# A four-layer graph network on one core: dinv as a row by 32x32 squares and two transfers, fewer state turns on TensorE, and a last mix and store chunk by chunk

## The chip, the cores and the metric

The kernel runs on one core of a Trainium2 chip. Time is device microseconds (us) of one execution, and the time of a kernel is the median over several executions. The core's engines work side by side, each through its own queue in order: TensorE (PE) multiplies and can turn (transpose) a 128x128 square, VectorE (DVE) and ScalarE (ACT) work element by element, GpSimd (POOL) does a few small operations here, and SyncE (SP) issues nearly all transfers, which land some time after their issue.

## The reference

32 graphs share one 512x512 adjacency matrix; each has 512 nodes of 128 features, in float32. There are four layers, each of the form x = x + layer(relu(layernorm(x))):

```python
# layer 0: graph convolution
A_hat = adj + eye(n); d = A_hat.sum(-1) ** -0.5
out = (d[:, None] * A_hat * d[None, :]) @ h @ W.T + b
# layer 1: gated graph network, five steps (in_matrix = out_matrix = adj)
m = adj @ h;  av = concat([m, m])
z = sigmoid(av @ w3.T + b3 + h @ u3.T + c3)
r = sigmoid(av @ w4.T + b4 + h @ u3.T + c3)
hv = tanh(av @ w5.T + b5 + (r * h) @ u5.T + c5)
h = (1 - z) * h + z * hv
# layers 2 and 3: graph attention, softmax over the edges
h = x @ W; e = leaky_relu((h @ a_src)[:, None] + (h @ a_dst)[None, :])
out = softmax(where(edge, e, -inf)) @ h        # layer 2: elu(out)
```

## The kernel before, in words

**An order laid out by a planner.** The program never writes its instructions down directly. `op` (line 61) notes an operation with its engine, an assumed cost, a due time and what it reads and writes. `Plan.run` (line 92) then plays the whole list through a model of the five engines (`attempt`, line 154): each engine takes, among its ready operations whose buffers are free, the one with the smallest due. A due is replaced by a smaller one if the chain of work behind an operation is long; the pairs in `ends` (line 305) say by how much, several are tried, and the order with the earliest end is emitted. So each engine's order is fixed when the program is built, and on the chip each engine waits in that order. `near_end` is the planned time after which a second way of setting dues applies. `IDLE_FROM` allows PE filler turns late in the plan; the profile shows none.

**Graphs in pairs.** Graphs are taken two at a time. `begin(b)` runs layer 0 for b and b+1 (`gcn`), `ggnn` the five steps of layer 1, and `attention` layers 2 and 3 (`gat`). Six lanes of graphs are in work at once, so that PE has other graphs' work while one waits. The planner takes one unit of due for 10.3 us (SLOT).

**Layer 0.** Graphs 0 to 3 (`first`) use the adjacency as it is: `product` (line 659) multiplies the four chunks of y by the rows of adjT, and adds the identity either by a fifth piece of 128 columns per chunk (graph 0, `by_diag` false) or by taking the diagonal block from `diag`, in which the identity has been added on DVE (graphs 1 to 3). dinv, the inverse square root of the degrees, is folded into the normalization and the output. Later pairs use the normalized matrix anT made by `normalized` (line 677). For that dinv is needed as a row along the free dimension: line 685 turns the four columns of dinv, each spread over 128 columns, into a PSUM bank `drow`, and four operations on DVE (line 690) multiply adjT by the column and the row, four more (line 693) fix the diagonal. `right_factors` (line 399) makes four combined blocks of a matrix on DVE, for the `products` of a pair (line 604), which take 28 instructions of 256 columns (line 628) for two graphs.

**Layer 1.** A state is kept as features by nodes (hT). Each step needs it as nodes by features (h) as well. There are two ways. By PE: `to_features` (line 554) does four turns (line 560) into a bank, and ACT copies them out (line 796). By squares: `shuttle` (line 564) lets DVE turn 32x32 squares (lines 570 and 574), SP writes them out in four transfers `far<-sq` (line 577), and one or two more, `h<-far` (line 581), read them back with the squares in place. `EARLY` (line 23) says from which due on (line 789) states go by squares. `FAR0`, `FAR1` (line 24) say for which graphs the very first state is turned that way (`shuttle_first`, line 589, four transfers out and four back), and not by PE and an ACT copy (line 746).

**Layers 2 and 3.** For the last four graphs (`near`) attention avoids transfers. Its last part mixes: for each of four blocks j, `mix_from` (line 903) multiplies e[j] into all four chunks c of the output, two chunks to a bank. Then for each bank a reciprocal (line 917), for layer 3 two scaled additions (line 925), and a store of two chunks (line 947).

Of the kernel before, what the change touches and what calls it, by code (L numbers as in the profile page):

```python
# [22 lines left out]
EARLY = 8  # L23
FAR0, FAR1 = 2, 4
# [231 lines left out]
def gnn_stack(ctx: ExitStack, tc: tile.TileContext, a: dict, out: bass.AP):  # L256
# [48 lines left out]
    }, [(179, 0.06), (175, 0.06), (177, 0.12)], 1350,  # L305
# [52 lines left out]
    op("DVE", 0.2, -15, lambda: nc.vector.tensor_scalar_add(b0.t, b0.t, -1.0), w=[b0])  # L358
# [6 lines left out]
    for l, w in ((2, "L2_gnn_W"), (3, "L3_gnn_w")):  # L365
        w_aug[l] = fixed([P, D + 3], f"w_aug{l}", 2)
        op("SP", 0.45, -990.5, lambda l=l, w=w: nc.sync.dma_start(w_aug[l].t[:, :D], a[w]), w=[w_aug[l][0]], delay=3.4)
        a_pair[l] = fixed([P, 2], f"a_pair{l}", 2)
        for i, k in enumerate(("src", "dst")):
            op("SP", 0.45, -990.4, lambda l=l, i=i, k=k: nc.sync.dma_start(  # L370
                a_pair[l].t[:, i:i + 1], column(a[f"L{l}_gnn_a_{k}"])), w=[a_pair[l][i]], delay=2.4)
# [23 lines left out]
    for m in range(C):  # L395
        op("DVE", 0.16, -6, lambda m=m: nc.vector.tensor_add(diag.t[:, m, :], block(adjT.t, m), ident.t),
           r=[adjT, ident], w=[diag[m]])
# [16 lines left out]
    of_adj = right_factors(adjT, -5)  # L414
# [38 lines left out]
    w0T = transposed(-9.2, (one(w0), 1), then=turned)  # L453
    gates = transposed((-700, -9.5, -700, -9.5), (halves("w4"), 1), (one(raw["u3"]), 1), (halves("w3") + halves("w4", minus), 1), (halves("w5"), 1), then=turned)
    u5T = transposed(-9.4, (one(raw["u5"]), 0.5), then=turned)
    gats = transposed(-4, (one(w_aug[2]), 1), (one(w_aug[3]), 1))
# [9 lines left out]
    for i, l in enumerate((2, 3)):  # L466
        p = Val("bank")
        op("PE", 0.3, -3, lambda i=i, l=l, p=p: nc.tensor.matmul(p.t[:, 0, :2], gats.t[:, i, :], a_pair[l].t, start=True, stop=True),
           r=[gats, a_pair[l]], w=[p])

        def columns(l=l, p=p):
            for j, (s, f) in enumerate(((1, SLOPE), (1, 1.0 - SLOPE), (0, SLOPE - 1.0))):
                nc.vector.tensor_scalar_mul(w_aug[l].t[:, D + j:D + j + 1], p.t[:, 0, s:s + 1], f)
        op("DVE", 0.3, 10, columns, r=[p], w=[w_aug[l][1]])
# [184 lines left out]
    def product(h, due, by_diag):  # L659

        p, m = Val("bank"), Val("m")
        for c in range(C):
            def times(c=c):
                row = adjT.t[:, c, :]
                if by_diag:
                    terms = [(0, c, row[:, :c * P]), (c, c + 1, diag.t[:, c, :]), (c + 1, C, row[:, (c + 1) * P:])]
                else:
                    terms = [(0, C, row), (c, c + 1, ident.t)]
                terms = [t for t in terms if t[0] < t[1]]
                for k, (lo, hi, right) in enumerate(terms):  # L670
                    nc.tensor.matmul(flat(p.t)[:, lo * P:hi * P], h.t[:, c, :], right, start=c == k == 0,  # L671
                                     stop=c == C - 1, skip_group_check=True)
            op("PE", MM if by_diag else MM + 0.1, due, times, r=[h[c], adjT, diag[c] if by_diag else ident], w=[p, m])
        op("ACT", A, due, lambda: nc.scalar.copy(flat(m.t), flat(p.t)), r=[p], w=[m])
        return m

    def normalized(begun):

        anT = fixed([P, C, N], "anT", C)
        drow = Val("bank")  # L680
        dinv2 = fixed(SMALL, "dinv2")

        def turn_dinv():
            for c in range(C):
                nc.tensor.transpose(drow.t[:, c, :], dinv.t[:, c:c + 1].to_broadcast([P, P]), ident.t)
        op("PE", C * TURN, -2, turn_dinv, r=[dinv, ident, begun], w=[drow])
        op("DVE", 0.1, -790, lambda: nc.vector.tensor_mul(dinv2.t, dinv.t, dinv.t), r=[dinv], w=[dinv2])

        for m in range(C):
            op("DVE", 0.7, -1, lambda m=m: nc.vector.scalar_tensor_tensor(  # L690
                anT.t[:, m, :], adjT.t[:, m, :], dinv.t[:, m:m + 1], flat(drow.t), op0=ALU.mult, op1=ALU.mult),
               r=[adjT, dinv, drow], w=[anT[m]])
            op("DVE", 0.26, -1, lambda m=m: nc.vector.scalar_tensor_tensor(
                block(anT.t, m), ident.t, dinv2.t[:, m:m + 1], block(anT.t, m), op0=ALU.mult, op1=ALU.add),
               r=[ident, dinv2], w=[anT[m]])
        return anT, right_factors(anT, 0, True)
# [4 lines left out]
    def gcn(pair, due):  # L701
        first, ys = pair[0] < 4, []
        for i, b in enumerate(pair):
            y = Val("y", C) if first else Val("pair", 2)
            if b == 0:
                norm_first(b, y)
            else:
                norm_relu(b, y, -797 if b == 1 else due + i, dinv if first else None)
            op("DVE", V, due + i + 1, lambda b=b: nc.vector.tensor_add(
                xs[b].t, xs[b].t, b0.t[:, None, :].to_broadcast([P, C, D])), r=[b0], w=[xs[b]])  # L710
            ys.append(y)

        ms = [product(y, due + i, pair[i] > 0) for i, y in enumerate(ys)] if first else products(*ys, factors["an"], due + 1)
        if b == 1:
            factors["anT"], factors["an"] = normalized(ms[0])
        for i, (b, m) in enumerate(zip(pair, ms)):
            p = Val("bank")

            def out_mm(m=m, p=p):
                for c in range(C):  # L720
                    nc.tensor.matmul(p.t[:, c, :], m.t[:, c, :], w0T.t[:, 0, :], start=True, stop=True)  # L721
            op("PE", C * MM1, due + i + 1.5, out_mm, r=[m, w0T], w=[p])
            if first:
                for c in range(C):
                    op("DVE", 0.26, due + i + 1.5, lambda b=b, c=c, p=p: nc.vector.scalar_tensor_tensor(
                        xs[b].t[:, c, :], p.t[:, c, :], dinv.t[:, c:c + 1], xs[b].t[:, c, :], op0=ALU.mult, op1=ALU.add),
                       r=[p, dinv], w=[xs[b][c]])
            else:
                op("DVE", V, due + i + 1.5, lambda b=b, p=p: nc.vector.tensor_add(flat(xs[b].t), flat(xs[b].t), flat(p.t)),
                   r=[p], w=[xs[b]])  # L730
# [4 lines left out]
    def ggnn(pair, due):  # L735
        hs, hTs, lanes = [], [], []
        for b in pair:
# [3 lines left out]
            norm_relu(b, h, due - 3)  # L741
# [68 lines left out]
    def masks(begun):  # L810

        maskT = {l: fixed([P, Q, N], f"maskT{l}", C, dtype=BF16) for l in (2, 3)}
        for l in (2, 3):
            far = Val(None, C)
            far.t = tiles(1, [Q, W, C, N], f"far_mask{l}", dram, BF16)[0]
            for c in range(C):
                part = Val("mask", 1)
                edges(l, c, part, lambda part=part: part.t, 14 + l, begun)
                op("SP", 0.4, 14 + l, lambda c=c, far=far, part=part: nc.sync.dma_start(
                    far.t[:, :, c, :].rearrange("q i n -> (q i) n"), part.t), r=[part], w=[far[c]], delay=2.2)  # L820
# [10 lines left out]
    def gat(b, l, due):  # L831
# [65 lines left out]
        ps, rden, v, n = (Val("bank"), Val("bank")), Val("rden", 2), Val("v", 2), Val("r", 2)  # L897
        if near:

            for j in range(C):  # L900
                def mix_from(j=j):
                    for c in range(C):
                        nc.tensor.matmul(flat(ps[c // 2].t).rearrange("p (c k) -> p c k", c=2)[:, c % 2, :D + 1],  # L903
                                         e.t[:, j, c * P:(c + 1) * P], h.t[:, j, :D + 1], start=j == 0 and c % 2 == 0,
                                         stop=j == C - 1, skip_group_check=True)
                op("PE", C * MM1, due + 4, mix_from, r=[e[j], h[j // 2], h[2 + j // 2]], w=[*ps])
        for a, p in enumerate(ps):
            pt = lambda p=p: flat(p.t).rearrange("p (c k) -> p c k", c=2)
            some = slice(2 * a, 2 * a + 2)
# [7 lines left out]
            op("DVE", 0.08, due + 4, lambda some=some, pt=pt: nc.vector.reciprocal(rden.t[:, some], pt()[:, :, D]), r=[p], w=[rden[a]])  # L917
            if l == 2:
                op("DVE", 0.335, due + 4, lambda some=some, pt=pt: nc.vector.tensor_mul(
                    v.t[:, some], pt()[:, :, :D], rden.t[:, some, None].to_broadcast([P, 2, D])), r=[p, rden[a]], w=[v[a]])  # L920
            else:
                def finish(a=a, pt=pt):
                    for c in range(2):
                        i = 2 * a + c
                        nc.vector.scalar_tensor_tensor(xb.t[:, i, :], pt()[:, c, :D], rden.t[:, i:i + 1], xb.t[:, i, :],
                                                       op0=ALU.mult, op1=ALU.add)
                op("DVE", 2 * 0.26, due + 4, finish, r=[p, rden[a]], w=[xb[2 * a], xb[2 * a + 1]])
# [17 lines left out]
        elif near:  # L945
            for a in range(2):
                op("SP", 0.45, due + 4, lambda a=a: nc.sync.dma_start(
                    out[b].rearrange("(c p) d -> p c d", p=P)[:, 2 * a:2 * a + 2], xb.t[:, 2 * a:2 * a + 2]),
                   r=[xb[2 * a], xb[2 * a + 1]])
# [4 lines left out]
    def begin(b):  # L954
        gcn((b, b + 1), STEPS * b - (16 if b == 2 else 10))
# [59 lines left out]
```

## Time and profile before

| | us |
|---|---|
| median of 6 runs (lowest, highest) | 1623.47 (1623.17, 1624.03) |
| the profiled execution | 1623.73 |
| its span, first to last instruction | 1622.0 |

The engines over that span: VectorE is busy 85% of it, ScalarE 45% and GpSimd 9%; the 16 DMA engines move 157.72 MB. The granted TensorE clock is 1.00 over the span. TensorE's first instruction starts at 1.05 us and its last one ends at 1617.9 us.

How to read it: in a group row ("| 7.2, 273 | 0.0") stand the engine's busy time in us, the mean ns of one instruction, and the idle time before them. In a wait row stand the total in us, the number of times and the longest. In a timeline row stand the start and the length in us, and at its end the number of instructions that were merged into it. A float32 matmul of 128 rows is two instructions on PE; a turn is one. Ends of PE instructions are modelled, since they overlap; starts are recorded. SPq is the issuing of transfers by SP.

### The profile page before, as it was taken

The page shows a single profiled execution, that of the slowest core. Times are in us where ns is not written, and L with a number is a line of the kernel's source. Part 1 is how long each engine was busy: PE and PEld are TensorE (multiplying, and loading weights), DVE is VectorE, ACT ScalarE, POOL GpSimd, SP SyncE. Part 2 cuts the span into 40 slices and gives each one's busy share as a digit, 9 for nine tenths or more (in the row PEclk, how much of TensorE's full clock was granted, in tenths as well). Part 3 has the DMA queues.
Part 4 walks back from the last instruction along what each step waited for, and adds up shares of the span by engine and source line. Part 5 has one row for each costly group of instructions (what it writes and reads, how often), then busy time and mean ns, then how long its engine had stood idle before and what let it go on. Part 6 is the DMA issues. An engine that isn't in the chain of part 4 may idle for free.

```text
span 1622.0 us, 24004 instructions
## 1 busy us (share of the span) xinstructions
PE 1614.0 (100%) x7326; PEld 1167.7 (72%) x7326; DVE 1378.1 (85%) x3971; ACT 725.0 (45%) x1628; POOL 145.7 (9%) x137
## 2 busy tenths in 40 slices
PE   9999999999999999999999999999999999999998
PEld 7666667776776767767777776767767686677778
DVE  8968688889888898888898888988888788888888
ACT  5644453535345353453544345343453524443554
POOL 2200000111001110001010011000010000000100
PEclk9999999999999999999999999999999999999999
DMA  4134243544535344353543535345353343444101
GB/s 131 26 78 116 67 114 88 132 102 99 125 79 136 92 106 116 89 130 82 129 106 91 137 80 123 99 98 130 85 128 88 85 99 79 104 98 111 40 22 52
DMA packets 374177, 157.72 MB, mean 97 GB/s; under 512 B 201664, under 2 KB 355616, under 8 KB 374048
## 3 DMA queue, kind: packets, MB, share of 16 engines
q1 hardware_dynamic: 373760, 155.67, 39.3%
q8 instruction: 58, 0.95, 0.3%
q14 instruction: 71, 0.58, 0.1%
q10 hardware_dynamic: 288, 0.52, 0.1%
HBM read 86.25 MB, written 69.84 MB: 96 GB/s over the span
## 4 chain that ended last, share of the span: by engine, by line
PE 94%; DVE 3%; DMA 1%; ACT 0%; POOL 0%; issue 0%; SPq 0%; DVEq 0%; ACTq 0%; POOLq 0%
PE bank L628 33%; PE bank L914 12%; PE bank L762 8%; PE bank L763 8%; PE bank L776 8%; PE bank L777 8%; PE bank L769 8%; PE bank L852 3%; PE bank L721 2%; PE bank L903 2%; PE bank L671 1%; PE bank L560 1%; DVE st L480 0%; DMA e<-in_adj_dram 0%; POOL rstd L493 0%
## 5 line engine op out<-in xcount | busy, mean ns | idle before, releaser
L493 POOL TENSOR_TENSOR rstd<-ve,mhalf 128x4 f32<-128x4 f32 x119 | 134.6, 1132 | 1381.9 <-DVE ve L485 1240.8
L628 PE MATMUL bank<-made,S 128*128 128x256 f32 x960 | 230.7, 380 | 0.5 <-DVE m L641 0.3
L914 PEld LDWEIGHTS bank<-h_gat,e 128*128 128x128 f32 x1792 | 210.7, 191 | 12.7 <-issue 10.5
L633 ACT COPY half<-bank 128x256 f32<-128x256 f32 x282 | 104.5, 371 | 243.7 <-PE bank L628 239.8
L914 PE MATMUL bank<-h_gat,e 128*128 128x129 f32 x1792 | 212.3, 275 | 0.0
L628 PEld LDWEIGHTS bank<-made,S 128*128 128x128 f32 x960 | 184.2, 196 | 31.3 <-issue 12.5
L765 ACT ACTIVATE r<-bank,gate_bw 128x512 f32<-128x512 f32 x160 | 109.6, 685 | 206.1 <-PE bank L763 188.2
L781 DVE TENSOR_TENSOR hv<-hv,hT 128x512 f32<-128x512 f32 x160 | 109.2, 683 | 81.9 <-ACT hv L779 81.6
L767 DVE SCALAR_TENSOR_TENSOR rh<-r,hT 128x512 f32<-128x512 f32 x160 | 109.7, 686 | 67.2 <-ACT r L765 65.7
L762 PE MATMUL bank<-m,wT 128*128 128x512 f32 x320 | 163.6, 593 | 0.1
L776 PE MATMUL bank<-m,wT 128*128 128x512 f32 x320 | 163.5, 592 | 0.0
L777 PE MATMUL bank<-rh,wT 128*128 128x512 f32 x320 | 163.4, 592 | 0.0
L763 PE MATMUL bank<-hT,wT 128*128 128x512 f32 x320 | 163.4, 592 | 0.0
L769 PE MATMUL bank<-m,wT 128*128 128x512 f32 x320 | 163.1, 592 | 0.0
L779 ACT ACTIVATE hv<-bank,gate_bw 128x512 f32<-128x512 f32 x160 | 109.5, 685 | 119.8 <-PE bank L777 119.8
L894 DVE SCALAR_TENSOR_TENSOR e<-row,h_gat,maskT 128x512 f32<-128x512 f32 x224 | 160.7, 741 | 0.0
L628 PE MATMUL bank<-adjT,h 128*128 128x256 f32 x640 | 159.7, 380 | 0.0
L628 PEld LDWEIGHTS bank<-adjT,h 128*128 128x128 f32 x640 | 123.0, 196 | 25.9 <-issue 14.4
L641 DVE TENSOR_TENSOR m<-half,bank 128x256 f32<-128x256 f32 x282 | 115.7, 412 | 26.8 <-PE bank L628 15.6
L771 ACT ACTIVATE z<-bank,gate_bw 128x512 f32<-128x512 f32 x160 | 109.4, 684 | 42.8 <-PE bank L769 39.8
L480 DVE BATCH_NORM_STATS2 st<-x 128x6 f32<-128x128 f32 x480 | 115.9, 279 | 7.2 <-DMA x<-in_x_dram 6.9
L777 PEld LDWEIGHTS bank<-rh,wT 128*128 128x128 f32 x320 | 60.8, 190 | 76.5 <-issue 66.2
(146 smaller groups left out, 2364.4 us busy)
## 6 DMA issues: line engine op xcount, KB each, us to landing
far<-sq SPq DMA_DIRECT2D x920, 64.0 KB
h<-far SPq DMA_DIRECT2D x240, 128.0 KB
gT<-far SPq DMA_DIRECT2D x56, 256.0 KB
row<-line SPq DMA_DIRECT2D x56, 256.0 KB
x<-in_x_dram SPq DMA_DIRECT2D x32, 256.0 KB
h<-far SPq DMA_DIRECT2D x28, 256.0 KB
out_dram<-x SPq DMA_DIRECT2D x28, 256.0 KB
hT<-far SPq DMA_DIRECT2D x104, 64.0 KB
```

Source lines behind the costliest of these rows:

```text
L480: op("DVE", 0.21, due, lambda c=c: nc.vector.bn_stats(st.t[:, c, :], xb.t[:, c, :]), r=[xb[c]], w=[st[c]])
L493: op("POOL", 1.0, due, lambda: nc.gpsimd.tensor_tensor(rstd.t, ve.t, mhalf.t, ALU.pow), r=[ve, mhalf], w=[rstd])
L628: nc.tensor.matmul(low(r), u[:, l, :], factors[k][0]()[:, l, :], start=fresh and l == 0, stop=l == 1, skip_group_check=not fresh)
L641: op("DVE", HV, due - 5, lambda: nc.vector.tensor_add(out(), u.t, low(t)), r=[u, t], w=[o])
L762: nc.tensor.matmul(flat(gate.t), gates.t[:, 0, :], flat(m.t), start=True, stop=False)
L763: nc.tensor.matmul(flat(gate.t), gates.t[:, 1, :], flat(hT.t), start=False, stop=True)
L767: op("DVE", V, due - 5, lambda: nc.vector.scalar_tensor_tensor(flat(rh.t), flat(r.t), 1.0, flat(hT.t), op0=ALU.add, op1=ALU.mult), r=[r, h ...
L769: op("PE", MM, due + 0.3, lambda: nc.tensor.matmul(flat(gate.t), gates.t[:, 2, :], flat(m.t), start=False, stop=True, skip_group_check=Tru ...
L776: nc.tensor.matmul(flat(cand.t), gates.t[:, 3, :], flat(m.t), start=True, stop=False)
L777: nc.tensor.matmul(flat(cand.t), u5T.t[:, 0, :], flat(rh.t), start=False, stop=True)
L894: op("DVE", 0.68, due + 3, lambda j=j: nc.vector.scalar_tensor_tensor(e.t[:, j, :], rows(row.t), h.t[:, j, D + 1:D + 2], mask(j), op0=ALU. ...
L914: nc.tensor.matmul(pt()[:, c, :D + 1], e.t[:, j, i * P:(i + 1) * P], h.t[:, j, :D + 1], start=(j == 0), stop=(j == C - 1))
```

## The change

- `product` always takes the diagonal from `diag`, for graph 0 too; `diag` is made early (due -800 and later in place of -6).
- dinv becomes a row in SBUF. POOL clears a small tile, DVE copies dinv into its last column of each square and turns the squares, SP writes the row of each square to DRAM (`line`) and reads it back spread over 128 partitions (`drow`). The operations on anT, not the turn, now wait for `begun`, graph 0's product.
- `EARLY` goes from 8 to 6, `FAR1` from 4 to 2.
- For the last graph's layer 3 (`apart`) blocks 0 and 1 are mixed into all chunks as before, then blocks 2 and 3 chunk by chunk; each chunk has a bank, a reciprocal, an addition and a store of its own.
- Many due times and the planner's ends change.

```diff
-EARLY = 8
-FAR0, FAR1 = 2, 4
+EARLY = 6
+FAR0, FAR1 = 2, 2
-    }, [(179, 0.06), (175, 0.06), (177, 0.12)], 1350,
+    }, [(175, 0.12), (173, 0.07)], 1400,
-    op("DVE", 0.2, -15, lambda: nc.vector.tensor_scalar_add(b0.t, b0.t, -1.0), w=[b0])
+    op("DVE", 0.2, -38.7, ...)
-        op("DVE", 0.16, -6, lambda m=m: nc.vector.tensor_add(diag.t[:, m, :], block(adjT.t, m), ident.t),
+        op("DVE", 0.26, -800 + 0.7 * m, ...)
-    of_adj = right_factors(adjT, -5)
+    of_adj = right_factors(adjT, -3.6)
-    w0T = transposed(-9.2, (one(w0), 1), then=turned)
-    gates = transposed((-700, -9.5, -700, -9.5), ...)
-    u5T = transposed(-9.4, (one(raw["u5"]), 0.5), then=turned)
-    gats = transposed(-4, (one(w_aug[2]), 1), (one(w_aug[3]), 1))
+    w0T = transposed(-11.7, ...)
+    gates = transposed((-700, -9.5, -700, -15.8), ...)
+    u5T = transposed(-15.2, ...)
+    gats = transposed(-0.4, ...)
...
-    def product(h, due, by_diag):
+    def product(h, due):
...
-                if by_diag:
-                    terms = [(0, c, row[:, :c * P]), (c, c + 1, diag.t[:, c, :]), (c + 1, C, row[:, (c + 1) * P:])]
-                else:
-                    terms = [(0, C, row), (c, c + 1, ident.t)]
+                terms = [(0, c, row[:, :c * P]), (c, c + 1, diag.t[:, c, :]), (c + 1, C, row[:, (c + 1) * P:])]
...
-        drow = Val("bank")
-        def turn_dinv():
-            for c in range(C):
-                nc.tensor.transpose(drow.t[:, c, :], dinv.t[:, c:c + 1].to_broadcast([P, P]), ident.t)
-        op("PE", C * TURN, -2, turn_dinv, r=[dinv, ident, begun], w=[drow])
+        column, four, line, drow = Val("four"), Val("four"), Val("line"), Val("row")
+        op("POOL", 0.2, -795, lambda: nc.gpsimd.memset(column.t, 0.0), w=[column])
+        op("DVE", 0.1, -790, lambda: nc.vector.tensor_copy(column.t[:, :, W - 1], dinv.t), r=[dinv], w=[column])
+        op("DVE", 0.2, -790, lambda: nc.vector.transpose(four.t, column.t), r=[column], w=[four])
+        op("SP", 0.4, -995, lambda: nc.sync.dma_start(line.t.rearrange("c q i -> q c i"), four.t[W - 1::W]), r=[four], w=[line], delay=3)
+        op("SP", 0.4, -995, lambda: nc.sync.dma_start(
+            drow.t, line.t.rearrange("c q i -> (c q i)").unsqueeze(0).to_broadcast([P, N])), r=[line], w=[drow], delay=5)
...
-            op("DVE", 0.7, -1, lambda m=m: nc.vector.scalar_tensor_tensor(
-                anT.t[:, m, :], adjT.t[:, m, :], dinv.t[:, m:m + 1], flat(drow.t), op0=ALU.mult, op1=ALU.mult),
-               r=[adjT, dinv, drow], w=[anT[m]])
+            op("DVE", 0.7, 3.2, lambda m=m: nc.vector.scalar_tensor_tensor(
+                anT.t[:, m, :], adjT.t[:, m, :], dinv.t[:, m:m + 1], drow.t, op0=ALU.mult, op1=ALU.mult),
+               r=[adjT, dinv, drow, begun], w=[anT[m]])
-        return anT, right_factors(anT, 0, True)
+        return anT, right_factors(anT, -16.5, True)
...
-            op("DVE", V, due + i + 1, lambda b=b: nc.vector.tensor_add(       # x + b0
+            op("DVE", V, due + i + 3.8, ...
-            op("PE", C * MM1, due + i + 1.5, out_mm, r=[m, w0T], w=[p])
+            op("PE", C * MM1, due + i + 3.3, out_mm, r=[m, w0T], w=[p])
-            norm_relu(b, h, due - 3)
+            norm_relu(b, h, due - 2)
-                edges(l, c, part, lambda part=part: part.t, 14 + l, begun)
+                edges(l, c, part, lambda part=part: part.t, -2.7 + l, begun)
...
+        apart = near and l == 3 and b == B - 1
+        per = 1 if apart else 2
+        ps, rden, v, n = [Val("bank") for _ in range(C // per)], Val("rden", C), Val("v", 2), Val("r", 2)
...
+            for js, cs in [([j], range(C)) for j in range(2 if apart else C)] + [((2, 3), [c]) for c in range(C if apart else 0)]:
+                op("PE", len(js) * len(cs) * MM1, due + 4, lambda js=js, cs=cs: mix_from(js, cs), ...)
...
-            for a in range(2):
+            for a in range(0, C, per):
                 op("SP", 0.45, due + 4, lambda a=a: nc.sync.dma_start(
-                    out[b].rearrange("(c p) d -> p c d", p=P)[:, 2 * a:2 * a + 2], xb.t[:, 2 * a:2 * a + 2]),
-                   r=[xb[2 * a], xb[2 * a + 1]])
+                    out[b].rearrange("(c p) d -> p c d", p=P)[:, a:a + per], xb.t[:, a:a + per]), r=[xb[c] for c in range(a, a + per)])
...
-        gcn((b, b + 1), STEPS * b - (16 if b == 2 else 10))
+        gcn((b, b + 1), STEPS * b - (13.8 if b == 2 else 10))
```

## The prediction

> **What bounds the kernel now.** I read the page's busy table and slices first, then what TensorE (PE) waited for, then the starts of consecutive PE instructions in the timeline, and last the DVE and SP rows at the end.
>
> ```profile
> PE 1614.0 (100%) x7326; PEld 1167.7 (72%) x7326; DVE 1378.1 (85%) x3971; ACT 725.0 (45%) x1628; POOL 145.7 (9%) x137
> PE bank L340 <- DVE hv L333: 1.1, 1, 1.1
> PE bank L628 <- ACT half L633: 0.9, 2, 0.5
> PE bank L628 <- DVE m L641: 0.6, 2, 0.3
> PE bank L903 <- DVE e L894: 0.5, 1, 0.5
> PE bank L383 <- DMA e<-in_adj_dram: 0.4, 1, 0.4
> PE bank L628 <- DVE S L616: 0.2, 1, 0.2
> ```
>
> The six waits are all that PE had: 3.7 us, of which 1.1 is the start. "Busy" is a modelled end, so I test it by pitch, the distance between one start and the next. A pair of 512-column instructions costs 0.86 us to the next start (75.28 to 76.14), a turn 0.11, early and late alike. Summing each pitch above the median of its group gives some 6.6 us lost in all: 1.4 before 10 us, 3.9 between 49 and 400 us, 1.2 in the last 20. So PE is bound by its own work; what is taken off it comes off the time, unless something else is then late.
>
> **PE work removed.** The rows that price it:
>
> ```profile
> 9.45 1.10 PE L671 MATMUL bank<-adjT,y 128*128 128x512 f32 x2
> ...
> 13.85 0.39 PE L438 MATMUL bank<-ident,u 128*128 128x128 f32 x2
> ...
> 14.96 0.39 PE L671 MATMUL bank<-v,y 128*128 128x128 f32 x2
> ...
> 18.46 0.72 PE L721 MATMUL bank<-wT,m 128*128 128x128 f32 x5
> 29.46 0.60 PE L685 MATMUL bank<-ident,dinv 128*128 128x128 f32 x4
> 29.90 0.51 PE L468 MATMUL bank<-a_pair,wT 128*128 128x2 f32 x4
> 73.98 0.60 PE L560 MATMUL bank<-ident,hT 128*128 128x128 f32 x4
> 74.42 1.02 PE L776 MATMUL bank<-m,wT 128*128 128x512 f32 x2
> 1286.62 1.11 PE L560 MATMUL bank<-ident,h 128*128 128x128 f32 x8
> 1287.56 0.39 PE L628 MATMUL bank<-adjT,h 128*128 128x256 f32 x1
> ```
>
> Columns: start, us, engine, line; the cost is the next start minus this one.
> - Graph 0's product with the extra identity takes 13.85 - 9.45 = 4.40 us; graph 1's with the diagonal 18.46 - 14.96 = 3.50. Graph 0 now does the second: -0.90.
> - The dinv turn: 29.90 - 29.46 = -0.44.
> - EARLY 8 to 6 takes the turns of graphs 0 and 1 after step 1 (due 6 and 7; those at due 0 and 1 stay): 2 x (74.42 - 73.98) = -0.88.
> - FAR1 4 to 2 takes the first turns of graphs 28 and 29: 1287.56 - 1286.62 = -0.94.
>
> Sum -3.16 us. Here the Trainium skill (TensorE: Matmul & The Clock Gate, Part 4: PE-mode transpose) gives about 275 ns for a turn inside a kernel. The records agree as durations (273 ns mean for L560 on hT), but the pitch is 110 ns, as turns overlap. By the rule the 20 turns would be 5.5 us and the sum 6.4; by the pitch 2.26 and 3.16. Back to back the pitch is what PE pays; I take it.
>
> **What replaces it.** The skill's VectorE: DVE Perf Modes (Rules for kernel authors) speaks against this: a 128x128 transpose belongs on TensorE, since VectorE turns only 32x32 blocks. The trace's price of the other way is two DVE transposes (0.77 us for both) and six transfers per state, and this is the nearest case, graph 2:
>
> ```profile
> 78.80 0.69 DVE L784 SCALAR_TENSOR_TENSOR hT<-hv,hT 128x512 f32<-128x512 f32 x1
> 79.53 0.77 DVE L570 STREAM_TRANSPOSE sq<-hT 128x256 f32<-128x256 f32 x2
> 80.33 1.78 SPq L577 DMA_DIRECT2D far<-sq  x4
> 83.62 1.30 SPq L581 DMA_DIRECT2D h<-far  x2
> ```
>
> From state (79.49) to the second h issue (84.34) is 4.85, and a transfer of this kind lands 2.3 us after its issue (the chain of waits has 2.31 for an hT): 7.2 us. Graph 1's step-1 state is done at 76.25, so its h comes at 83.4 rather than at 78.3. The step-2 products of graphs 0 and 1 start on PE at 84.35. Their first 1.73 us need graph 0 alone; S[1], three DVE sums of 0.42 later, would be there at 84.7 and is used at 86.08. Slack 1.4. PE will be 2.2 us ahead here (0.90 + 0.44 + 0.88), the state 1.34: slack 0.5. SP issues nothing between 57 and 80.3 us, so its queue is free; graph 2's squares come behind and are late by about 1.4 us, but its products start only at 108. I take 0; if the queue is in a bad order, 3 (below), and all of PE stands behind that matmul. By the rule PE would keep 0.88 us and DVE save 1.5; DVE is 82% busy there, so PE is the dearer.
>
> Graphs 28 and 29: hT is first read at their step-0 gates, after 28 product instructions of 0.216 (6.0 us) and whatever stands between; 26 graphs already go this way and no PE wait is on an hT transfer. Two more DVE transposes of 0.43 and eight issues each (3.8 us of SP), two ACT copies of 0.59 less. DVE is 72% busy from 1280 to 1300. Taken 0, bound 0 to +1: a late hT.
>
> dinv as a row: one POOL memset (0.1, POOL sits idle till 7.99), one DVE copy (0.15, as the dinv product at L687) and one transpose (0.30, as L887): 0.45 us on DVE near 11 us, before x statistics. Two issues on SP (0.4 each) ahead of the x loads; the second waits for the first to land (about 2.3), with w_aug and x loads behind it. x of graphs 2 and 3 are read from 11.9 on, the rest from 24 us. The row is wanted at 31.7, so it has 15 us. Taken 0; between 0 and +0.8, if graph 2 and 3's statistics come late. A bank is free from 29.5 to 35: a gain of up to 0.5.
>
> diag early: four DVE sums, 0.28 each, go ahead of graph 1's statistics, so its y (ACT from 12.51) comes 0.8 late. PE leaves graph 0's product at 12.9, has 1.1 us of weight turns, and wants y at 14.0: y's first chunk is there at 13.7. Zero.
>
> The dues (begin(2), anT from -1 to 3.2, x + b0, masks, the matmuls for w_aug) change no amount of work. DVE is the engine they relieve or starve: it is 28.76 of 29 us busy from 31 to 60. Bounds: the 3.9 us lost between 49 and 400 may go to half (-2); or PE may wait more (+3). I take 0.
>
> **The end.** Each row the last of its kind:
>
> ```profile
> 1617.94 0.17 DVE L917 RECIPROCAL rden<-bank 128x2 f32<-128x2 f32 x1 [0.22 <-PE bank L903]
> 1618.03 1.11 DVE L925 SCALAR_TENSOR_TENSOR x<-bank,rden,x 128x128 f32<-128x128 f32 x4
> 1618.65 0.37 SPq L947 DMA_DIRECT2D out_dram<-x  x1
> 1619.17 0.37 SPq L947 DMA_DIRECT2D out_dram<-x  x1
> ```
>
> After PE's last matmul four sums run on DVE, and the last store goes out at 1619.17. With a bank per chunk only one reciprocal and one sum are left: a store follows its last sum's start by 0.37 (1618.28 to 1618.65), so 1618.03 + 0.37 = 1618.40, -0.77. But SP issues 0.52 apart and chunks finish 4 x 0.112 = 0.45 apart, so three of them slip it by 0.2: -0.56. The smaller transfer (64 KB for 128) gains 0 to 0.2. I take -0.6. e[3] is ready at 1615.4 and wanted at about 1616.0 (16 instructions of graph 30 and 16 of graph 31 at 0.112 after 1612.38). The two more banks that the last mix takes could hold it up: 0 to +0.5; by then no other graph is left to want them, so 0.
>
> **Sum.** -3.16 - 0.6 = -3.8. The profiled execution took 1623.73 (span 1622.0 and 1.7 around it): 1619.9. The median of the runs is 0.26 lower, so 1619.7.
>
> **Rivals.**
> - *Removed and passed on* (0.5): 1619.7, own range 1618.8 to 1620.6.
> - *Stalls go too* (0.19): dues and the freed bank take 2 us of the stalls at 49 to 400: 1617.7. For: the waits at L633, L641 and L616 are of products with nothing beside them. Against: no edit touches their chain directly.
> - *The start eats it* (0.22): shuttled states or statistics come late, or DVE holds PE back before 110 us: 1 to 3 us of new idle, 1621.7. For: DVE is full from 31 to 60, and graph 3's h was issued 6.5 us after its squares (88.30 to 94.83), not 3.3, behind other squares in SP's queue. With that, graph 1's slack of 0.5 becomes a wait of 2.7.
> - *Put-off factors* (0.09): anT and the sums on it, some 7 us of DVE, slip behind other work on the full DVE, and graphs 4 and 5's first product (6.0 us of PE, begun at 48.96) is not there to fill PE. Up to 6 us idle, 1619.7 + 6 = 1625.7, slower. It decides from 3.8 us of new idle. Against: the order is laid out with PE's work in view, so other graphs' steps fill part.
> - *Turns hidden anyway*: not, as the pitch shows.
>
> Measurement can't tell 0.2%, 3.2 us, from no change, so "faster" is below 1620.2. The first case gives 0.40 there, the second 0.19, the third 0.06: 0.65. Slower (above 1626.7) 0.04; the rest, 0.31, is within. The range, 1617.3 to 1622.8, leaves out the fourth case and a tail of the second.
>
> **What would show it.** L685 and L671's identity rows gone; L560 with 40 turns on hT for 48 and 16 on h for 24; 3.1 to 3.2 us less PE work by pitch; the last store 0.5 to 0.6 us after PE's end plus 0.1. Wrong if PE's waits grow by over 1 us, most likely at 82 to 86 or 48 to 60.

## The result, and the profile after

| | before | after |
|---|---|---|
| median of the runs | 1623.59 | 1619.44 |
| lowest and highest | 1623.04, 1625.72 | 1619.3, 1619.8 |
| span of the profiled execution | 1622.0 | 1617.7 |

The ratio is 0.9974, with a 95% interval of 0.9967 to 0.9981. In a later set the changed kernel took 1619.66 against 1623.20 (0.9976, 0.9966 to 0.9986). The forecast was 1619.7. The gain is 3.5 to 4.2 us, a quarter of one per cent.

The page's busy line after the change, and what PE waited for (us in total, times, longest):

```profile
PE 1610.9 (100%) x7310; PEld 1165.6 (72%) x7310; DVE 1382.0 (85%) x3983; ACT 721.7 (45%) x1622; POOL 144.9 (9%) x138
```

```profile
PE bank L628 <- ACT half L633: 1.4, 3, 0.5
PE bank L340 <- DVE hv L333: 1.1, 1, 1.1
PE bank L720 <- ACT m L633: 0.5, 1, 0.5
PE bank L905 <- DVE e L893: 0.2, 1, 0.2
```

PE has 16 instructions less (20 turns gone, 4 more in graph 0's product, whose pieces are smaller), and it is as full as before. The waits are not the same ones: those on L641 and L616 are gone, two on a copy by ACT (L633) have come. (A second profiled execution of the changed kernel, after_again below, has one wait on L641 again, 0.3 us; the waits on L633 are the same.)

To compare runs I split each span in three. *Work* counts every PE instruction at its pitch, the usual distance from its start to the next: 0.429 us for 512 columns, 0.324, 0.216 and 0.112 for 384, 256 and 128 to 131, 0.109 for a turn (0.120 for a turn of an h), 0.213 for the 16 instructions of the run-up, which multiply a tile of zeros before any data is there. *Waits* are what is left between PE's first and last start, so they hold small delays too that the profile's list of waits does not name. *After PE* is the rest of the span. The first start is at 1.05 everywhere.

| profiled execution | work | waits | after PE | span |
|---|---|---|---|---|
| before | 1609.2 | 7.5 | 4.2 | 1622.0 |
| after | 1606.1 | 7.2 | 3.4 | 1617.7 |
| difference | -3.1 | -0.3 | -0.8 | -4.2 |

So three quarters of the gain is PE work, a fifth is the end, and the waits came out even. That is the sum of the prediction, nearly term by term. But even is a total, and the waits moved. PE's busy time by stretch shows where (a row has the stretch in us from the span's start and its length, then busy time and number of instructions of PE, its weight loads, DVE, ACT and POOL, and last the granted clock, the share of DMA and GB/s). Before:

```profile
31.00:60.00 29.00, 28.79 (x118) 21.56 (x118) 28.76 (x108) 17.50 (x45) 5.19 (x5) 1.00 0.19 37
110.00:500.00 390.00, 389.09 (x1623) 272.27 (x1622) 321.38 (x884) 170.13 (x365) 29.92 (x26) 1.00 0.42 101
```

After:

```profile
31.00:60.00 29.00, 28.07 (x109) 19.68 (x109) 28.34 (x116) 17.25 (x42) 7.22 (x6) 1.00 0.20 37
110.00:500.00 390.00, 390.00 (x1619) 272.09 (x1618) 322.51 (x890) 171.62 (x366) 27.89 (x27) 1.00 0.42 103
```

By busy time PE idles 0.7 us more from 31 to 60, and 0.9 less from 110 to 500, where it is now full. Since the ends of PE instructions are modelled, busy time shows only part of a wait. Counted as *waits* above, in us:

| stretch | 0 to 31 | 31 to 49 | 49 to 400 | 400 to 1500 | 1500 to the end |
|---|---|---|---|---|---|
| before | 1.9 | 0.0 | 3.7 | 0.4 | 1.6 |
| after | 1.2 | 1.6 | 1.8 | 0.6 | 2.0 |

So some 2 us went from 49 to 400, and about as much came elsewhere. The new waits of the start, in the timeline of PE after the change:

```profile
31.06 1.98 PE L628 MATMUL bank<-made,S 128*128 128x256 f32 x8
33.50 1.14 PE L628 MATMUL bank<-made,S 128*128 128x256 f32 x4 [0.46 <-ACT half L633]
35.10 1.14 PE L628 MATMUL bank<-adjT,S 128*128 128x256 f32 x4 [0.46 <-ACT half L633]
```

Eight instructions from 31.06 are done with their pitch at 32.79 (31.06 + 8 x 0.216), but the next starts at 33.50, and its group runs 0.11 longer: some 0.8 us for one wait. It is in the product of a pair of graphs: the next piece adds onto a bank that ACT has to copy out first. A product with nothing beside it waits there. One with other PE work in between does not have to; a case of that is shown under g2 below. That detail matters for what follows.

### The profile page after: what moved, and what is told of

It is laid out like the page before. It is cut to its first block, busy times and chain, and to the rows that moved or that the text cites. A ratio compares the mean times of both kernels' runs of the same rounds, so it can differ in the third digit from the quotient of the medians.

```text
span 1617.7 us, 24009 instructions
## 1 busy us (share of the span) xinstructions
PE 1610.9 (100%) x7310; PEld 1165.6 (72%) x7310; DVE 1382.0 (85%) x3983; ACT 721.7 (45%) x1622; POOL 144.9 (9%) x138
## 4 chain that ended last, share of the span: by engine, by line
PE 97%; DVE 2%; DMA 0%; ACT 0%; issue 0%; ACTq 0%; DVEq 0%
PE bank L628 35%; PE bank L919 12%; PE bank L761 8%; PE bank L775 8%; PE bank L776 8%; PE bank L762 8%; PE bank L768 8%; PE bank L851 3%; PE bank L720 2%; PE bank L668 1%; DVE e L893 1%; PE bank L905 1%; PE bank L560 0%; DVE x L929 0%; DMA e<-in_adj_dram 0%; DVE st L534 0%
## 5 line engine op out<-in xcount | busy, mean ns | idle before, releaser
L633 ACT COPY half<-bank 128x256 f32<-128x256 f32 x282 | 104.3, 370 | 244.1 <-PE bank L628 243.2
L641 DVE TENSOR_TENSOR m<-half,bank 128x256 f32<-128x256 f32 x282 | 115.7, 412 | 18.1 <-ACT half L633 8.8
L762 PEld LDWEIGHTS bank<-hT,wT 128*128 128x128 f32 x320 | 60.8, 190 | 76.5 <-issue 75.3
```

What stands on the lines that cost most here:

```text
L641: op("DVE", HV, due - 5, lambda: nc.vector.tensor_add(out(), u.t, low(t)), r=[u, t], w=[o])
L762: nc.tensor.matmul(flat(gate.t), gates.t[:, 1, :], flat(hT.t), start=False, stop=True)
```

## The experiments

Differences below are between medians of the same set of runs. First each part alone, put into the kernel before, with its old dues.

**p1_diag**: graph 0's product by diag, diag early.

```diff
-    op("DVE", 0.16, -6, ...diag...)
+    op("DVE", 0.26, -800 + 0.7 * m, ...diag...)
-    ms = [product(y, due + i, pair[i] > 0) ...]
+    ms = [product(y, due + i) ...]
```

> The kernel before with one part of the change: graph 0's product takes its diagonal from diag, which is made early. Theory (PE is bound by its own work, and a part is worth its pitch): 0.9 us less than before, about 1622.7, with PE's work lower by 0.9 and its waits within 0.7 of before. Rival 1 (the gain came with the new dues and planner ends, and a part alone only shifts waits): within 0.3 us of before. Rival 2 (DVE holds the start back, so early sums on DVE cost what PE saves): PE's waits before 110 us up by 0.9.

**p2_row**: dinv as a row; its new function from the change, anT's due as before.

> The kernel before with one part of the change: dinv becomes a row by squares and two transfers, dues as before. Theory: 0.44 us less, about 1623.1, no PE wait on anT or on the row. Rival 1: within 0.3 us of before either way. Rival 2 (the row comes late, because its second transfer waits in SP's queue or delays the x loads): a wait of DVE on the row or on x that reaches PE, 0.5 to 1 us more than before.

**p3_squares**:

```diff
-EARLY = 8
-FAR0, FAR1 = 2, 4
+EARLY = 6
+FAR0, FAR1 = 2, 2
```

> The kernel before with one part of the change: the states of graphs 0 and 1 after step 1, and the first states of graphs 28 and 29, go by squares (EARLY 6, FAR1 2), dues as before. Theory: 1.8 us less, about 1621.8; PE's work lower by 1.8, no new wait on an h or hT transfer. Rival 1: within 0.3 us of before. Rival 2 (latency of the squares in the start): a PE wait of 1 to 3 us between 75 and 110 us, so 1622 to 1625.

**p4_tail**: the last mix, sums and stores chunk by chunk (`apart`), the rest as before.

> The kernel before with one part of the change: the last graph's last mix and store chunk by chunk, dues as before. Theory: 0.6 to 0.8 us less, about 1622.8, all of it between PE's last matmul and the end of the span (4.2 us before, 3.4 to 3.6 here), PE's own work unchanged. Rival 1: the store queue or the four banks take it back, within 0.3 us of before.

| part alone | median, to before | ratio, 95% | work | waits | after PE |
|---|---|---|---|---|---|
| p1_diag | 1623.96, +1.0 | 1.0006 (0.9998 to 1.0014) | 1608.4 | 8.2 | 4.2 |
| p2_row | 1624.45, +1.5 | 1.0008 (0.9999 to 1.0016) | 1608.7 | 9.6 | 4.1 |
| p3_squares | 1625.31, +2.3 | 1.0016 (1.0010 to 1.0023) | 1609.0 | 8.9 | 4.7 |
| p4_tail | 1623.41, +0.4 | 1.0002 (0.9994 to 1.0011) | 1609.4 | 9.8 | 3.3 |

None gained; p3_squares is slower beyond its interval. My theory had 0.4 to 1.8 us less for each, and the first rival had each within 0.3 us of before: both missed. The work did fall in p1 and p2 (by 0.8 and 0.4, as forecast), and p4's end is 0.9 shorter, but the waits took it back.

In p3 the planner found PE short of work near the end and put in 15 filler turns (1.6 us), so the work hardly fell, and what is left after PE grew by 0.5. Its second rival, squares that come late in the start, did not happen: PE loses nothing there between 75 and 110 us. Between 500 and 1500 us its waits are 3.7 us, against 0.3 in before, far from the states of graphs 0 and 1.

In p1 two waits are new: PE waited 0.5 us for the load of w_aug, whose turns had moved forward, and a third time for a copy at L633. The change moves just those turns back (due -4 to -0.4) and counts the load as longer (3.4 to 5), and in the changed kernel that wait is absent; these two edits were not tried by themselves.

In p2 the second rival came true: the row came late. SP issued its transfer at 19.96 us, behind six loads of x, and DVE waited for it; a sum on x that stood behind that on DVE then kept a bank from PE:

```profile
25.66 0.75 DVE L692 SCALAR_TENSOR_TENSOR anT<-adjT,dinv,row 128x512 f32<-128x512 f32 x1 [1.25 <-DMA row<-line]
30.66 0.38 PE L468 MATMUL bank<-a_pair,wT 128*128 128x2 f32 x2 [0.41 <-DVE x L727]
```

With two more waits for a copy at L633, this makes up most of the 2.1 us that PE waits in p2 above before. The changed kernel has no wait for the row.

(The waits column is of one execution; 1.5 of p4's 9.8 are a late adjacency, told of at the end. The medians carry the verdict.)

So is the part not worth its work, or does the new order spoil it? Each part makes the planner lay out everything anew. The next pair keeps every engine's order.

**g1_left_out**: the order of before, the removed PE work just not issued (ACT's copies of the turns stay, and those parts of the result are not computed).

```diff
-                    terms = [(0, C, row), (c, c + 1, ident.t)]
+                    terms = [(0, C, row)]
-            for c in range(C):
+            for c in ():
                 nc.tensor.transpose(drow.t[:, c, :], dinv...)
-            p = to_features(new, due + 2, ...)
+            p = to_features(new, due + 2, ..., left_out=b < 2 and s == 1)
-                p = to_features(h, due - 2, hT)
+                p = to_features(h, due - 2, hT, left_out=b in (28, 29))
```

> The order of the kernel before, with the PE work that the change removes simply not done and nothing in its place: graph 0's identity pieces, the dinv turn, the two step-1 state turns of graphs 0 and 1, the two first turns of graphs 28 and 29 (so these parts of the result are left out); every engine's order stays. Theory A (PE is bound by its own work; parts alone failed because each lays the order anew): 3.1 us less than before, PE's waits within 0.5 of before. Theory B (the removed work stood beside waits that end when they end, so it is hidden): 0 to 1.5 us less, with PE's waits up by the difference, before 110 us.

**f1_put_back**: the order of the changed kernel, with as much work put back. Graph 0's product is issued with the identity pieces again, and candidate's function issues turns into the bank that it then overwrites:

```diff
         def candidate():
+            if b < 2 and s == 1 or b in (28, 29) and s == 0:
+                for c in range(C):
+                    nc.tensor.transpose(cand.t[:, c, :], hT.t[:, c, :], ident.t)
+            if b == 0 and s == 0:
+                for c in range(C):
+                    nc.tensor.transpose(cand.t[:, c, :], dinv.t[:, c:c + 1].to_broadcast([P, P]), ident.t)
```

> The order of the changed kernel, with the removed PE work put back beside it: graph 0's product with the identity pieces, and five extra groups of four turns (one of dinv, four of states) ahead of candidate matmuls of graphs 0, 1, 28 and 29. Theory A: 3.1 us more than the changed kernel, by the pitch of 0.11 a turn; by the duration of 0.27 a turn it would be 6.4. Theory B: 0 to 1.5 us more, PE's waits lower by the difference.

**g2_more_left_out**: the order of the changed kernel, with six more turns of four left out:

```diff
-            p = to_features(new, due + 2, ...)
+            p = to_features(new, due + 2, ..., left_out=b < 2 and s == 0)
-                p = to_features(h, due - 2, hT)
+                p = to_features(h, due - 2, hT, left_out=True)
```

> The order of the changed kernel, with 2.8 us more of PE work not done and nothing in its place: the state turns of graphs 0 and 1 after step 0 and the four first turns of graphs 0, 1, 30 and 31 that are still PE's (these parts of the result are left out). Theory A (PE is bound by its own work): 2.8 us less than the changed kernel. Theory E (an order is laid so that the other engines are only just ahead of PE: work added is paid in full, as the put-back run showed, work removed under it turns into waits, as the left-out run showed): 0 to 1 us less, PE's waits up by 2 to 3.

Its base, the changed kernel once more, **after_again**:

> The changed kernel once more, as the base for the three others of this set: 4.0 to 4.3 us less than before.

| order kept | work | waits | median, to its base |
|---|---|---|---|
| g1_left_out, to before | -3.2 | +3.0 | 1623.18, -0.3 (ratio 0.9996, 0.9988 to 1.0004) |
| f1_put_back, to after | +3.0 | +2.2 | 1622.80, +2.9 to +3.5 |
| g2_more_left_out, to after_again | -2.8 | +2.0 | 1619.35, -0.3 |

Work and waits are of one profiled execution, so they need not add up to the difference of the medians. All of f1's +2.2 of waits lies before 13 us, in the load of the adjacency, and its profiled execution is its slowest. f1 was not in one set with the changed kernel: it took 0.65 less than before (0.9996, 0.9988 to 1.0004), the changed kernel 4.15 and 3.54 less in its two sets, hence +2.9 to +3.5. after_again itself was expected 4.0 to 4.3 below before and came to 3.54. g2's profiled execution is the fastest of its 8, so the waits of a usual one are nearer +2.5.

Work added to the changed kernel is paid in full. Work left out gives, by the medians, about a tenth of its size, in both orders; g1's interval leaves room for 1.9 of 3.2 us, not for all of it. So theory A is right upwards, as far as one order shows, and wrong downwards. The price upwards also settles the two prices of a turn: by the pitch f1 was to pay 3.1, by the duration 6.4, and it pays about 3.

Read as a square, these runs show that neither half gains much by itself. Less PE work in the old order (g1): -0.3 to before. The old amount of PE work in the new order (f1): -0.65, about what the shorter end gives. Less work in the new order (the changed kernel): -3.5 to -4.2.

Where the left-out work goes can be read at one place. The changed kernel (after_again), at the first turns of the last two graphs (start, length, engine, line):

```profile
1380.08 2.75 PE L628 MATMUL bank<-made,S 128*128 128x256 f32 x12
1382.66 1.11 PE L560 MATMUL bank<-ident,h 128*128 128x128 f32 x8
1383.61 1.04 PE L628 MATMUL bank<-adjT,S 128*128 128x256 f32 x4
```

g2_more_left_out, the same place:

```profile
1379.53 2.75 PE L628 MATMUL bank<-made,S 128*128 128x256 f32 x12
1382.74 1.14 PE L628 MATMUL bank<-adjT,S 128*128 128x256 f32 x4 [0.46 <-ACT half L633]
```

The eight turns took 0.95 (1382.66 to 1383.61). Without them the first and the second group of pieces start 3.21 apart (1379.53 to 1382.74) and not 3.53, and the second group runs 0.1 longer: 0.2 gained of 0.95. The turns had stood in the gap in which ACT copies the bank; they were cover, not only cost. The turns of graphs 28 and 29 show it too. Before, with the turns ahead of the first row (0.94 us):

```profile
1287.56 1.04 PE L628 MATMUL bank<-adjT,h 128*128 128x256 f32 x4
1288.44 1.03 PE L628 MATMUL bank<-made,h 128*128 128x256 f32 x4
```

g1_left_out:

```profile
1286.89 1.03 PE L628 MATMUL bank<-adjT,h 128*128 128x256 f32 x4
1288.17 1.14 PE L628 MATMUL bank<-made,h 128*128 128x256 f32 x4 [0.25 <-DVE m L641]
```

In before these two groups are 0.88 apart, here 1.28: 0.4 of the 0.94 is lost at once, to a DVE sum that had just been in time. Theory B had g1's new waits before 110 us; only about half of them are there. Some stand far from any edit (0.5 us on ACT's z near 767 us), and what makes those was not traced. A wait can also come with the execution: after_again has one of 0.3 us near 1213 us that the first execution of the same kernel has not.

If a fixed order gives the work back, the order and its dues should be the other half of the change.

**q1_parts_old_dues**: all four parts, with the dues, the load delay and the planner ends of before.

> All four parts of the change, with the due times, load delay and planner ends of the kernel before. Theory A: the work is 3.1 us less, but the order is a new one, and its waits decide: between before and before plus 2, as with the parts alone, so 2 to 5 us above the changed kernel. Theory C (the parts help only together, the dues are small): within 1 us of the changed kernel.

**q2_dues_alone**: these alone.

> The due times, load delay and planner ends of the change alone, none of its four parts. Theory A: the dues fit the changed work and not this one, so the time is within 2 us of before, either side, by new waits. Theory D (the gain is the dues', the parts are worth nothing): 3 to 4 us less than before.

q1 took 1625.47, 2.0 more than before (1.0012, 1.0006 to 1.0019); q2 1626.19, 2.7 more (1.0018, 1.0011 to 1.0025), and 2 at most was expected of it. Each half is slower beyond its interval, and together they are some 4 us faster. q1 has the work of the changed kernel to the instruction, 1606.1, and waits of 11.8. The first two lines of what PE waited for in q1:

```profile
PE bank L628 <- ACT half L633: 3.3, 7, 0.5
PE bank L628 <- DVE m L641: 1.3, 3, 0.8
```

Seven waits for a copy in a product, where the changed kernel has three. Does the gain hang on these dues in particular?

**n1_one_due**: the changed kernel with one due back, of two products that cost 0.44 us of PE together.

```diff
-        op("PE", 0.3, 9, ... a_pair ...)
+        op("PE", 0.3, -3, ... a_pair ...)
```

> The changed kernel with one due back at its old value, that of the two small products for w_aug's score columns (9 back to -3); no work is added or removed, but the planner moves some 540 of PE's 1,900 rows. Theory E (waits belong to an order, and another order draws others): 1 to 4 us more than the changed kernel, with PE's work the same to 0.5 us and the waits up. Rival (the waits are those of the work, not of the order): within 0.4 us of the changed kernel.

1622.75, 3.1 more than after_again, so of this set's gain of 3.54 only 0.45 is left with one due put back. The expectation of the same work to 0.5 us was missed a little: the planner put in 7 filler turns (0.8 us). The waits are 9.3 against 7.5, and five are for a copy in a product, where after_again has three:

```profile
PE bank L628 <- ACT half L633: 2.4, 5, 0.5
```

It is the order that carries the waits, not these operations. Seven plans were laid out anew in these experiments (p1 to p4, q1, q2 and n1), and PE waits longer in each, 8.2 to 11.8 us, than in before and the changed kernel, 7.2 to 7.5. (Without the load of the adjacency this still holds for all but p4.) Both kernels of the pair thus seem to have good orders among those that the planner makes; how their dues were found is not on record.

**b1_two_queues**: an attempt on the end, in the same order.

```diff
+                queue = nc.scalar if apart and a % 2 == 0 else nc.sync
-                op("SP", 0.45, due + 4, lambda a=a: nc.sync.dma_start(
+                op("SP", 0.45, due + 4, lambda a=a, queue=queue: queue.dma_start(
```

> The changed kernel in the same order, with the last graph's stores of chunks 0 and 2 issued by ACT, so that SP's 0.5 us between issues no longer holds up the last store. PE's work and waits as in the changed kernel; after PE's last matmul 0.1 to 0.3 us less, so 0.1 to 0.3 us less in all. Rival (the landing of the last store, or ACT's slower issue, ends last): no difference.

1620.10, 0.4 more than after_again; 0.1 to 0.3 less was expected, and the rival had no difference. First the changed kernel's end:

```profile
1614.63 0.16 DVE L922 RECIPROCAL rden<-bank 128x1 f32<-128x1 f32 x1
1614.83 0.35 DVE L929 SCALAR_TENSOR_TENSOR x<-bank,rden,x 128x128 f32<-128x128 f32 x1
1613.78 1.77 SPq L951 DMA_DIRECT2D out_dram<-x  x4
```

And b1's two queues:

```profile
1613.75 1.32 ACTq L952 DMA_DIRECT2D out_dram<-x  x2
1614.21 1.31 SPq L952 DMA_DIRECT2D out_dram<-x  x2
```

The last store is issued at 1615.20 in the one (1613.78 + 1.77 less its own 0.35) and at 1615.17 in the other. It waits for the last sum (1614.83 + 0.37), not for SP, which had been free. What lies between the last issue and the end of the span grew from 2.5 to 2.9 us; the second queue is the only edit, but what in it takes the time was not traced. No run that computes the whole result beat the changed kernel.

## Why the prediction came out

**PE work, -3.16.** It measures -3.1 (1609.2 to 1606.1); graph 0's product is worth 0.82 by the pitches, not 0.90. The other pieces are right: 40 turns on hT and 16 on h, no identity rows, no dinv turn.

```profile
L560 PE MATMUL bank<-ident,hT x40: 272/273/328, 47.3 to 1570.0; 128*128 128x128 f32 x40
L560 PE MATMUL bank<-ident,h x16: 273/283/288, 26.0 to 1383.2; 128*128 128x128 f32 x16
```

The choice of the pitch over the duration was right too, as f1 showed. The 275 ns that the prediction took from the Trainium skill (TensorE: Matmul & The Clock Gate, Part 4: PE-mode transpose) is that page's figure for a bf16 square in one kernel's context; the float32 turns here last as long (273 ns), but they start 110 ns apart.

**The end, -0.6.** It measures -0.8. The last store comes 0.86 us after PE's last pitch and not 1.43: -0.56, the number forecast. But not for the reason given: the 0.2 that I took off for SP's spacing are on DVE. The sum starts 0.20 after its reciprocal (1614.63 to 1614.83), against 0.09 in before, and the reciprocal starts 0.29 after PE's last pitch, against 0.20. That the number is met to 0.01 is luck. The other 0.25 come after the issue (2.78 to 2.53), with a store of half the size; I had allowed 0 to 0.2.

**What replaces the turns, 0.** No PE wait is on a transfer of h or hT. The step-1 squares of graphs 0 and 1 go out from 70.5 us, the last h of the two is issued at 77.1, and their step-2 product starts at 82.1, without a wait and 5 us after that issue. The row of dinv is read from 24.9 us, and its transfer was issued at 19.0. This was closer than the 15 us of room that I gave it: in p2 the same transfer took 5.7 us (19.96 to 25.66), by which the room here would be some 0.25 us, an estimate from that one transfer.

**The waits, 0.** They measure -0.3 as a total, and here the number was right by an argument that the runs refute. The first part said that what is taken off PE comes off the time unless something else is late, and the list of rivals said "Turns hidden anyway: not, as the pitch shows". The pitch shows what a turn costs where it stands. It does not show what PE does when the turn is gone: g1 and g2 show that PE then mostly waits, for a copy or a sum that was only just in time. I also priced the dues at 0, as they "change no amount of work", with +3 and -2 for bounds. Without them (q1) the four parts cost 2.0 and do not save 4; given the parts, they are worth 5.6 to 6.2 us. The two errors are opposite, the work is worth less by itself and the dues more, and together they make the forecast sum. That is luck, as far as the argument of the prediction goes.

**The rivals.** *Stalls go too* happened at its place: the waits from 49 to 400 us fell from 3.7 to 1.8, near the 2 us forecast. f1 has 1.8 there too, and g1 4.5, so this came with the order and not with the work. *The start eats it* also happened in part, with 1.6 us of new waits from 31 to 49, though on ACT's copies, and not on late states or statistics. The two nearly cancelled. *Put-off factors* fell: anT began at 24.9 us, earlier than the 31.7 of before, for all that its due was later.

What stays open: which of the dues matter, and whether other orders of the changed work are better still. n1 shows one way to lose the gain; no run shows that 7 us of waits is the least.

## What to carry to other kernels

In an order laid out by a planner, a full engine was here a sign that added work is paid, and not that removed work is gained: look at what stands just behind the instruction that goes, and ask what the engine would then wait for. Judge a cut in work only together with an order made for it, and expect that a changed due can move as much time as the cut itself (3.1 us each, here). To price a part, keep the order and leave the work out or put it back; these two runs told more than four runs of parts alone.

## Not expected of the hardware

The load of the adjacency at the start is uneven from one execution to the next, at the same instructions. PE's 16 turns of it, in after_again and then in f1_put_back:

```profile
4.62 2.74 PE L383 MATMUL bank<-ident,e 128*128 128x128 f32 x16
```

```profile
6.96 2.82 PE L383 MATMUL bank<-ident,e 128*128 128x128 f32 x12 [0.55 <-DMA e<-in_adj_dram]
```

They were over at about 7.4 us in the one (4.62 + 2.74) and at 9.8 in the other (6.96 + 2.82), whose profiled execution, at 1624.77, is the slowest of its 13 (median 1622.80). p4's is its slowest too (1625.36, median 1623.41). One profiled execution can thus carry some 2 us that its median has not; for differences of this size the medians decide, and the profile tells only where.
